# A linear layer and a product of squares by one level of Strassen, in a kernel whose order a planner writes

## The chip, the cores and the metric

One core of one Trainium2 chip. The time is device microseconds of one execution; the kernel before takes 1416.3 us as the median of three runs (1412.21 to 1417.54). Engines are named as in the profile: PE (TensorE), DVE (VectorE), ACT (ScalarE), POOL (GpSimd) and SP (SyncE, which issues most DMAs).

## The reference

A factorization machine: a linear layer plus half the sum, over 64 embeddings, of the square of a product minus the product of the squares. All in fp32; x is 1024 x 512, weight 64 x 512 x 512.

```python
out_lin = x @ lin_w.T + lin_b
xv = jnp.einsum('bf,efm->bem', x, weight)
zp = jnp.einsum('bf,efm->bem', jnp.square(x), jnp.square(weight))
interaction = 0.5 * jnp.sum(jnp.square(xv) - zp, axis=1)
return out_lin + interaction
```

Nearly all the work is `xv`, 64 products of 1024 x 512 by 512 x 512. `zp` summed over e is one product only: the squares of x by the sum over e of the squared weights.

## The kernel before

The 512 output columns are cut into groups of 16, 16 and then twenty times 24; with 64 embeddings a column a group is 1024 or 1536 wide. For each group the product of x and the weights is done by Strassen's method in the form of Winograd, on two levels. The outer level takes seven products, in the order 1, 6, 5, 2, 7, 4, 3; each is again cut, by `tree` into seven products of two matmuls, or, for the products 1, 5 and 7 of the wide groups, by `wide_tree` into twenty products of 3 x 3 cells. Names that the profile's rows use: `X1` to `X7` are the sums of x for the outer products, made once at the head by copies (ACT) and sums; `w11`, `w12`, `w21`, `w22a`, `w22b` are the quarters of a group's weights, `T1a`, `T1b`, `T2` their outer sums (made by DMAs of POOL that add), `t` the inner sums of weights (POOL, L421); `oa` to `od` hold the results of outer products, `p5`, `p53` those of inner ones. `b1`, `b3`, `b2_0` and `b2_1` are four PSUM buffers of two banks (the profile leaves out numbers and shows `b`; `_l` and `_r` are their halves). A product leaves a bank by DVE, which adds another term (L421), or by a copy of ACT (L431), often into another bank in which a further product is added: such a copy must be done before that product begins.

Beside these products ACT squares each finished output (L438) and DVE sums it over the embeddings (L447) into `acc`. In the same way each quarter of the weights is squared into `wsq` and summed into `w2_sum`; the two halves of a quarter are two loads of SP (L452), two squares and two sums.

Around that: at the head the linear layer, 32 matmuls of 128x512 (L503), goes to `lin_dram`; at the end the product of -x²/2 (L916, on DVE) with `w2_sum`, 32 matmuls of 128x512 (L950), is added to acc and the linear part (L930, L421) and stored.

Nothing of the order is written by hand. Every step is added to `Plan` with a cost on its engine; for PE a key gives a preferred place. `Plan.order` makes due times backward from the products, moves them by the table `AHEAD_OF` (signs of steps with eighths of a microsecond), and then deals out the steps forward in a time of its own: each engine takes the one that is ready and due first. Each engine then works strictly in this order. The even and the odd wide groups share their signs, so the order repeats every two groups, 124.8 us.

## Time and profile before

| | |
|---|---|
| Median of three runs | 1416.3 us (1412.21 to 1417.54) |
| The profiled execution | 1415.96 us, span 1414.2 us, granted clock 0.997 |
| PE busy | 1396.6 us (99%) |
| POOL busy | 1173.7 us (83%) |
| DVE busy | 1100.0 us (78%) |
| ACT busy | 806.0 us (57%) |
| Moved by DMA | 251.76 MB, mean 178 GB/s |

A row of the timeline gives the start in us, the length, the engine, the line of the kernel, the operation, out<-in, shapes and the number of records; in brackets the idle time just before it and what ended that. A matmul in fp32 leaves two records. PEld is the load of the stationary operand, SPq and ACTq the DMA queues of these engines.

### The profile page before, as it was taken

What the parts mean: (1) busy time and instruction counts of PE and PEld (TensorE: products, weight loads), DVE (VectorE), ACT (ScalarE), POOL (GpSimd) and SP (SyncE); (2) the same over time, 40 slices, a digit from 0 to 9 for tenths busy, and PEclk for the clock granted to TensorE, in tenths of its full rate; (3) what the DMA queues carried; (4) which work ended last, traced back from release to release, by engine and by line L of the source; (5) the groups of instructions that cost most, each with busy time, mean ns of one, the idle gap of its engine ahead of it and who ended that gap; (6) DMA issues with size and microseconds to landing.
All of it is one profiled execution on the core that took longest, in us unless ns stands there. A gap on an engine that the chain in (4) does not pass through costs nothing.

```text
span 1414.2 us, 16647 instructions
## 1 busy us (share of the span) xinstructions
PE 1396.6 (99%) x5160; PEld 971.5 (69%) x5160; DVE 1100.0 (78%) x1461; ACT 806.0 (57%) x1293; POOL 1173.7 (83%) x1117
## 2 busy tenths in 40 slices
PE   8999989999999999999999999999999999999998
PEld 3887757767776766767676676777677677767663
DVE  2678678878878786887879688787968878796895
ACT  1456465656757465665656566565746556574642
POOL 5999978897979798797979879897987989788870
PEclk9999999999999999999999999999999999999999
DMA  8589596777949676795968678596958859694773
GB/s 260 164 192 227 135 202 153 165 188 161 228 120 228 160 178 171 167 223 117 230 159 192 160 180 208 131 222 146 216 143 195 197 132 221 135 238 109 163 193 112
DMA packets 92599, 251.76 MB, mean 178 GB/s; under 512 B 29472, under 2 KB 30496, under 8 KB 92512
## 3 DMA queue, kind: packets, MB, share of 16 engines
q0 software_dynamic: 26448, 134.49, 49.6%
q1 hardware_dynamic: 65488, 115.17, 24.0%
q8 instruction: 42, 0.69, 0.2%
q10 hardware_dynamic: 576, 1.05, 0.2%
q14 instruction: 45, 0.37, 0.1%
HBM read 127.04 MB, written 6.19 MB: 94 GB/s over the span
## 4 chain that ended last, share of the span: by engine, by line
PE 90%; POOL 4%; DMA 4%; DVE 1%; issue 1%; ACT 0%; SPq 0%; POOLq 0%; DVEq 0%; ACTq 0%
PE b L464 51%; PE b_r L464 18%; PE b_l L464 17%; POOL t L421 2%; PE b_r L950 1%; PE b_l L950 1%; DMA oc<-od 1%; DMA T<-T1a 1%; DMA oa<-xT 1%; PE b_l L503 1%; PE b_r L503 1%; DMA w<-weight 1%; POOL X L421 1%; DMA X<-xT 0%; POOL ob L456 0%
## 5 line engine op out<-in xcount | busy, mean ns | idle before, releaser
L464 PE MATMUL b<-t,X 128*128 128x384 f32 (+1 forms) x1504 | 518.5, 474 | 1.9 <-DVE ob L421 1.1
L464 PEld LDWEIGHTS b<-t,X 128*128 128x128 f32 x1504 | 276.1, 190 | 168.4 <-DVE oa L421 18.8
L421 POOL TENSOR_TENSOR t<-t,w 128x256 f32<-128x256 f32 (+1 forms) x200 | 232.6, 1287 | 9.0 <-PE b L464 5.7
L421 POOL TENSOR_TENSOR t<-w 128x768 f32<-128x768 f32 (+1 forms) x88 | 163.0, 1860 | 88.1 <-PE b_l L464 70.5
L438 ACT ACTIVATE oa<-oa 128x768 f32<-128x768 f32 (+1 forms) x176 | 142.8, 822 | 134.5 <-DVE oa L421 132.4
L464 PE MATMUL b<-w,X 128*128 128x384 f32 (+1 forms) x576 | 193.9, 469 | 0.1
L464 PE MATMUL b_l<-t,X 128*128 128x256 f32 x720 | 189.6, 381 | 3.9 <-ACT b_l L431 3.9
L464 PE MATMUL b_r<-t,X 128*128 128x256 f32 x600 | 167.9, 383 | 0.4 <-DVE ob L421 0.3
L447 DVE TENSOR_REDUCE acc<-oa 128x12 f32<-128x768 f32 (+1 forms) x176 | 161.6, 920 | 3.7 <-ACT oa L438 3.7
L447 DVE TENSOR_REDUCE w_sum<-wsq 128x12 f32<-128x768 f32 (+1 forms) x176 | 161.5, 920 | 1.1 <-ACT wsq L438 1.0
L464 PEld LDWEIGHTS b_l<-t,X 128*128 128x128 f32 x720 | 137.2, 191 | 32.2 <-ACT b_l L431 4.5
L464 PEld LDWEIGHTS b<-w,X 128*128 128x128 f32 x576 | 109.1, 190 | 56.5 <-ACT p L431 2.1
L464 PEld LDWEIGHTS b_r<-t,X 128*128 128x128 f32 x600 | 113.9, 191 | 47.7 <-issue 5.0
L438 ACT ACTIVATE wsq<-w 128x768 f32<-128x768 f32 (+1 forms) x132 | 107.3, 821 | 38.8 <-DVE w_sum L447 16.9
L421 DVE TENSOR_TENSOR oa<-b,oa 128x768 f32<-128x768 f32 (+1 forms) x88 | 82.0, 932 | 59.6 <-PE b L464 55.7
L421 POOL TENSOR_TENSOR t<-w,t 128x384 f32<-128x384 f32 (+1 forms) x96 | 107.7, 1122 | 2.4
L431 ACT COPY b<-b 128x768 f32<-128x768 f32 (+1 forms) x94 | 71.2, 757 | 60.3 <-PE b L464 58.0
L464 PE MATMUL b_r<-w,X 128*128 128x256 f32 x400 | 99.8, 380 | 0.0
L464 PE MATMUL b<-T,X 128*128 128x384 f32 (+1 forms) x264 | 91.3, 477 | 0.6 <-DMA T<-T1a 0.6
L421 DVE TENSOR_TENSOR oa<-b,oc 128x768 f32<-128x768 f32 (+1 forms) x66 | 61.2, 930 | 34.7 <-PE b L464 32.9
L464 PEld LDWEIGHTS b_r<-w,X 128*128 128x128 f32 x400 | 76.3, 191 | 14.3
L421 POOL TENSOR_TENSOR oc<-ob,p 128x512 f32<-128x512 f32 (+1 forms) x80 | 82.3, 1105 | 3.6 <-ACT p L431 2.0
(143 smaller groups left out, 2618.1 us busy)
## 6 DMA issues: line engine op xcount, KB each, us to landing
w<-weight SPq DMA_DIRECT2D x120, 384.0 KB, 6.0
ob<-od POOLq DMA_DIRECT2D x40, 768.0 KB, 7.9
oc<-od POOLq DMA_DIRECT2D x40, 768.0 KB, 9.5
T<-weight SPq DMA_DIRECT2D x40, 384.0 KB, 4.0
w<-T POOLq DMA_DIRECT2D x20, 768.0 KB, 6.5
T1a<-weight SPq DMA_DIRECT2D x20, 384.0 KB, 3.3
w22a<-weight SPq DMA_DIRECT2D x20, 384.0 KB, 8.8
T1a<-weight POOLq DMA_DIRECT2D x10, 768.0 KB, 11.9
```

The costliest lines, as they stand in the source:

```text
L421: return f(o.ap, a.ap, b.ap)
L431: return nc.scalar.copy(o.ap, i.ap)
L438: lambda _: nc.scalar.activation(o.ap, i.ap, AF.Square), i.atoms, o.atoms)
L447: nc.vector.tensor_reduce(o, x, axis=AX.X, op=ALU.add)
L464: nc.tensor.matmul(a.ap, b.ap, w.ap, start=start, stop=True, skip_group_check=True)
L503: nc.tensor.matmul(o[j].ap, x.ap[:, ts((g * 2 + j) % (NB // 2), P)], w.ap, start=(k == 0), stop=(k == NK - 1),)
L950: nc.tensor.matmul(z.ap, view(xe[h, k // KH])[:, k % KH, ts((g * 2 + j) % (NB // 2), P)], reg("w2_sum", k * M, M).ap, start=(k == 0), stop ...
```

## The change

Both the linear layer and the last product are cut by one level of the same scheme: seven products of eight matmuls of 128x256 instead of 32 of 128x512 (`outer_products`, `big`). The sums of lin_w are made by DVE and those of `w2_sum` by POOL; the sums of x for the linear layer are those that the groups need anyway, of which X5 and X7 are now put on DVE (POOL made them before). The squares of x move from DVE to ACT, the adding of acc and of the linear part goes by quadrants, and five stores replace eight. Two copies from bank to bank by ACT stand in each `outer_products`. The loads of lin_w go through the queue of ACT in quarters, those of x through SP, and the second half of x no longer through ACT.

Four matmuls of zeros (`WARM`), from a DVE memset, stand at the start of PE's order.

In the planner loads share one line with the adding DMAs (`queue`), with less cost for both; copies and squares cost ACT less. The table has new numbers. The rings `p5` and `p53` keep their two buffers.

```diff
+HALF = 0.5 ** 0.5
+WARM = 4
+P5S = 2
+P53S = 2
 AHEAD_OF = """
-0:l 1:hvhc 2:3bp 3:hvw0 4:37v 5:338 6:3g7 7:34e 8:1o 9:33e a:33f b:-d c:369 d:-2 e:28 f:1 g:-1v h:-k i:-2k
...
+0:-1d 1:28mt 2:1rdw 3:28qb 4:28sp 5:1rhs 6:1r1z 7:1o2z 8:r13 9:1ny7 a:3m5 b:1qhi c:1nqc d:1okx e:1qxc f:m62
...
-        plan.add({ACT: 0.19 + 0.00083 * o.size}, emit, i.atoms, o.atoms,
+        plan.add({ACT: 0.06 + 0.00083 * o.size}, emit, i.atoms, o.atoms,
                  banks=i.banks(False) + o.banks(True))
 
     def square(o, i):
-        plan.add({ACT: 0.22 + 0.00083 * o.size},
+        plan.add({ACT: 0.10 + 0.00083 * o.size},
                  lambda _: nc.scalar.activation(o.ap, i.ap, AF.Square), i.atoms, o.atoms)
 
     def reduce(o, i, writes):
-    def dma(o, i, reads, writes, cost=2.4, land=1.5, queue=nc.sync):
-        plan.add({SP: cost}, lambda _: queue.dma_start(o, i), reads, writes, land=land)
+    def dma(o, i, reads, writes, moves=1.3, land=1.8, queue=nc.sync):
+        plan.add({SP: 0.4}, lambda _: queue.dma_start(o, i), reads, writes, land=land, queue=moves)
 
     def dma_add(o, i, rows, reads, writes):
         def emit(_):
             nc.gpsimd.dma_start(o, i, accum_op=ALU.add)
 
-        plan.add({POOL: 1.0}, emit, reads + writes, writes, land=2.0, queue=3.1 * rows / 1024)
+        plan.add({POOL: 0.7}, emit, reads + writes, writes, land=1.8, queue=2.5 * rows / 1024)
...
-    for k in range(NK):
-        q, r = divmod(k, KH)
-        for h in range(2):
-            o = x_in(h, q, r)
-            dma(o.ap, x_src[:, k, ts(h, H)], (), o.atoms, 1.2, 2.0,
-                nc.sync if h == 0 else nc.scalar)
-        o = reg("ob", KH * H + k * M, M)
-        dma(o.ap, lw_src[:, k, :], (), o.atoms, 1.2, 2.0)
-
...
+    C = M // 2
+    lw_in(0, 0, nc.scalar)
+    x_load(0, 0, nc.sync, 2)
+    lw_in(1, 0, nc.scalar)
+    x_load(0, 1, nc.sync)
+    lw_in(0, 1, nc.scalar)
+    lw_in(1, 1, nc.scalar)
+    x_load(1, 1, nc.sync)
+    x_load(1, 0, nc.sync)
+
+    def big(o, x, w, first, key, parts=((0, 0, 4), (1, 0, 4))):
+
+        for n, (k, j0, j1) in enumerate(parts):
+            outs = [reg(o, j * C, C) for j in range(j0, j1)]
+            xs = [Reg(x.tile, x.off + k * H + j * P, P) for j in range(j0, j1)]
+
+            def emit(_, k=k, outs=outs, xs=xs, j0=j0):
                 return [
-                    nc.tensor.matmul(
-                        o[j].ap, x.ap[:, ts((g * 2 + j) % (NB // 2), P)], w.ap,
-                        start=(k == 0), stop=(k == NK - 1),
-                    )
-                    for j in range(2)
+                    nc.tensor.matmul(a.ap, b.ap, w(k).ap, start=first and k == 0 and j % 2 == 0,
+                                     stop=True, skip_group_check=True)
+                    for j, (a, b) in enumerate(zip(outs, xs), j0)
                 ]
 
-            plan.add({PE: 2 * mm_cost(N)}, emit, x.atoms + w.atoms, reg(b).atoms,
-                     key=-1000 + 4 * k + g, banks=o[0].banks(True) + o[1].banks(True))
-    for g, b in enumerate(lin_banks):
-        name, off = ("oc", g * 2 * M) if g < 3 else ("w22b", 0)
-        for j in range(2):
-            tt(reg(name, off + j * M, M), bank(b, j), bias)
-        o = reg(name, off, 2 * M)
-        dma(lin_dram[:, ts(g, 2), :].rearrange("p a m -> p (a m)"), o.ap, o.atoms, (("lin", g),))
+            plan.add({PE: (j1 - j0) * mm_cost(C)}, emit,
+                     sum((r.atoms for r in (*xs, w(k), *outs)), ()),
+                     sum((r.atoms for r in outs), ()), key=key + 0.1 * n,
+                     banks=sum((r.banks(True) for r in outs), ()))
+
+    zero = reg("t", 0, P + N)
+    plan.add({DVE: 0.8}, lambda _: nc.vector.memset(zero.ap, 0.0), (), zero.atoms)
+    for n in range(WARM):
+        z, o = reg("t", 0, P), bank(f"b2_{n // 2}", n % 2)
+        zw = reg("t", P, N)
+        plan.add({PE: 1.8 * mm_cost(N)},
+                 lambda _, z=z, o=o, zw=zw: nc.tensor.matmul(o.ap, z.ap, zw.ap, start=True, stop=True),
+                 zero.atoms, o.atoms, key=-2000 + n, banks=o.banks(True))
+
...
+    tt(two(lsum[1]), lw(0, 1, (M, KH)), lw(0, 0, (M, KH)), only=DVE)
+    tt(two(lsum[2]), lw(1, 1, (M, KH)), two(lsum[1]), only=DVE)
+    tt(two(lsum[4]), lw(1, 0, (M, KH)), two(lsum[2]), only=DVE)
+    tt(two(lsum[7]), lw(0, 1, (M, KH)), lw(1, 1, (M, KH)), only=DVE)
...
-    tt(x_block(5), x_in(1, 1), x_in(1, 0), True)
+    tt(x_block(5), x_in(1, 1), x_in(1, 0), True, DVE)
     minus_both(x_block(6), x_block(5), x_in(0, 0))
-    tt(x_block(7), x_in(0, 0), x_in(1, 0), True)
+    tt(x_block(7), x_in(0, 0), x_in(1, 0), True, DVE)
     minus_both(x_block(3), x_in(0, 1), x_block(6))
+
+    def outer_products(xs, ws, base_key, ready, leave):
+
+        u2, u3, m4, m5 = "b2_0", "b1", "b3", "b2_1"
+        big("b1", xs[1], ws[1], True, base_key)
+        copy(pair(u2), pair("b1"))
+        big("b1", xs[2], ws[2], False, base_key + 1)
+        leave(0, 0, "b1")
+        big(m4, xs[4], ws[4], True, base_key + 2)
+        ready(0, m4)
+        big(m5, xs[5], ws[5], True, base_key + 3)
+        ready(1, m5)
+        big(u2, xs[6], ws[6], False, base_key + 4)
+        copy(pair(u3), pair(u2))
+        big(u3, xs[7], ws[7], False, base_key + 5)
+        leave(1, 0, u3)
+        leave(1, 1, u3)
+        big(u2, xs[3], ws[3], False, base_key + 6, ((0, 0, 2), (1, 0, 2), (0, 2, 4), (1, 2, 4)))
+        leave(0, 1, u2)
+
...
-                dma(o.ap, source(g, q)[:, k * iw:(k + 1) * iw], (), o.atoms, 2.4 * iw / 1024)
+                dma(o.ap, source(g, q)[:, k * iw:(k + 1) * iw], (), o.atoms, 1.3 * iw / 1024)
...
-        plan.add(
-            {DVE: 1.24},
-            lambda _, x=x: nc.vector.scalar_tensor_tensor(
-                x.ap, x.ap, -0.5, x.ap, ALU.mult, ALU.mult
-            ),
-            x.atoms, x.atoms,
-        )
...
+    x2 = {(h, q): next(rooms) for h, q in ((0, 0), (0, 1), (1, 1), (1, 0))}
+    for (h, q), x in x2.items():
+        dma(x.ap.rearrange("p (a m) -> p a m", a=KH), x_src[:, ts(q, KH), ts(h, H)], (), x.atoms)
+        plan.add({ACT: 0.10 + 0.00083 * x.size},
+                 lambda _, x=x: nc.scalar.activation(x.ap, x.ap, AF.Square, scale=HALF),
+                 x.atoms, x.atoms)
...
+    tt(two(zsum[1]), w2(0, 1), w2(0, 0))
+    tt(two(zsum[2]), w2(1, 1), two(zsum[1]))
+    tt(two(zsum[4]), w2(1, 0), two(zsum[2]))
+    tt(two(zsum[7]), w2(0, 1), w2(1, 1))
...
+    def ready(c, b):
+        if c == 0:
+            tt(rest[1, 0], rest[1, 0], pair(b), True)
+        else:
+            tt(rest[1, 1], rest[1, 1], pair(b))
+            tt(rest[0, 1], rest[0, 1], pair(b))
+
+    def leave(h, c, b):
+        r = rest[h, c]
+        n = 1 if (h, c) != (0, 1) else 2
+        for k in range(n):
+            o = Reg(r.tile, r.off + k * 2 * N // n, 2 * N // n)
+            tt(o, o, reg(b, k * 2 * N // n, 2 * N // n), c == 0)
+            dma(out_dst[:, 4 * h + k * 4 // n:4 * h + (k + 1) * 4 // n, ts(c, C)],
+                o.ap.rearrange("p (a m) -> p a m", m=C), o.atoms, ())
+
+    outer_products(xs, ws, 1e6, ready, leave)
```

The steps of the periodic part are the same, in another order. Three places of it:

PE in a periodic pair of groups, where the first wide tree begins: `b3_r` and `b3_l` take the tree's first products, ACT copies `b3_r` to `b2_1_l`, and the next `b3_r` waits for that. Before:

```order
L464 MATMUL b3_r<-t_81,X1_62 128x256 [waits DVE_49]
L464 MATMUL b3_l<-t_81,X1_62 128x256 [waits Pool_49]
L464 MATMUL b3_l<-t_81,X1_62 128x256
L464 MATMUL b2_0<-t_81,X3_64 128x384 [waits DVE_49]
L464 MATMUL b2_0<-t_81,X3_64 128x384
L464 MATMUL b3_r<-t_81,X1_62 128x256 [waits Activation_49,Pool_49]
L464 MATMUL b2_1_l<-t_81,X1_62 128x256 x2
```

and now:

```order
L472 MATMUL b3_r<-t_81,X1_62 128x256 [waits DVE_49]
L472 MATMUL b3_l<-t_81,X1_62 128x256 [waits Pool_49]
L472 MATMUL b3_l<-t_81,X1_62 128x256
L472 MATMUL b3_r<-t_81,X1_62 128x256 [waits Activation_49,Pool_49]
L472 MATMUL b2_1_l<-t_81,X1_62 128x256 x2
```

Two matmuls of another tree, 128x384, have moved out of the gap between the product and the matmul that waits for its copy.

ACT in the first wide group (`w_71` is w21; `wsq_86` and `wsq_87` are the two buffers that take its halves' squares). Before:

```order
L438 ACTIVATE wsq_87<-w_69 128x768
L438 ACTIVATE wsq_86<-w_69 128x768
L438 ACTIVATE oa<-oa 128x2x384
L438 ACTIVATE ob<-ob 128x2x384
L438 ACTIVATE wsq_87<-w_71 128x768
L431 COPY b_1_l<-b_r 128x512
L438 ACTIVATE oa<-oa 128x2x384
```

and now:

```order
L446 ACTIVATE wsq_86<-w_71 128x768
L446 ACTIVATE ob<-ob 128x2x384
L446 ACTIVATE oa<-oa 128x2x384
L439 COPY b_1_l<-b_r 128x512
L439 COPY p_0_82<-b_l 128x512
L439 COPY b_1_r<-b_l 128x512
L439 COPY p_0_82<-b_r 128x256
L446 ACTIVATE ob<-ob 128x2x384
L438 ACTIVATE oa<-b_r 128x256
L446 ACTIVATE ob<-ob 128x2x384
L439 COPY b_0_l<-b_1_l 128x512
```

The square directly ahead of the copy was one of w21, its second half; now a square of w21, its first half, stands three rows ahead of the copy, and that of the other half comes some rows behind the last one shown.

The end of PE's order and of DVE's after the change (`w2_sum` times squares of x; X2, X5 and w12 hold what is stored). PE:

```order
L529 MATMUL b2_0<-T1a_74,X6_67 128x256 x8
L529 MATMUL b1<-w11_69,X1_62 128x256 [waits DMAHW5_49,Activation_49,Pool_49]
L529 MATMUL b1<-w11_69,X1_62 128x256 x7
L529 MATMUL b2_0<-w2_sum_90,T1b_75 128x256 x6
L529 MATMUL b2_0<-w2_sum_90,T1b_75 128x256 [waits DVE_49]
L529 MATMUL b2_0<-w2_sum_90,T1b_75 128x256
```

and DVE:

```order
L429 TENSOR_TENSOR w12_70<-w12_70,b2_1 128x1024 [waits DVE_49]
L429 TENSOR_TENSOR w12_70<-w12_70,b1 128x1024 [waits DVE_49,PE_49,Activation_49]
L429 TENSOR_TENSOR X2_63<-X2_63,b2_0 128x512 [waits PE_49]
L429 TENSOR_TENSOR X5_66<-X5_66,b1 128x1024
L429 TENSOR_TENSOR X2_63<-X2_63,b2_0 128x512 [waits PE_49]
```

Before, 32 matmuls stood here and a DVE sum of 512 columns followed each four; now product 7 waits for a copy of the product just before it, and the last product's seventh matmul for DVE.

337 lines of the change are left out of this document (193 added, 144 removed).

## The prediction

> **What bounds the kernel now.** I read the busy shares and the chain of waits first, then the busy time in windows cut at the program's stages, then the groups of waits of TensorE, and last the timeline at each place where TensorE stands idle. From the page:
>
> ```profile
> PE 1396.6 (99%) x5160; PEld 971.5 (69%) x5160; DVE 1100.0 (78%) x1461; ACT 806.0 (57%) x1293; POOL 1173.7 (83%) x1117
> PE 90%; POOL 4%; DMA 4%; DVE 1%; issue 1%; ACT 0%; SPq 0%; POOLq 0%; DVEq 0%; ACTq 0%
> ```
>
> TensorE is busy for 1396.6 of 1414.2 us: 17.6 us of idle time are all that better waiting could win, beside shorter products. The windows say where they lie (each row: the window, its length, busy time of PE, PEld, DVE, ACT and POOL, the granted clock, the DMA share, GB/s):
>
> ```profile
> 0.00:36.00 36.00, 30.45 (x66) 13.37 (x67) 8.18 (x13) 6.73 (x8) 21.11 (x28) 1.00 0.83 257
> 60.00:120.00 60.00, 58.97 (x267) 49.69 (x267) 47.02 (x74) 33.08 (x58) 57.66 (x68) 1.00 0.84 198
> 120.00:180.00 60.00, 59.25 (x229) 42.53 (x228) 43.68 (x65) 34.60 (x62) 58.16 (x65) 1.00 0.72 171
> 180.00:200.00 20.00, 16.09 (x51) 11.07 (x50) 12.43 (x16) 10.45 (x17) 16.00 (x16) 0.83 1.01 227
> 300.00:424.80 124.80, 124.80 (x466) 87.18 (x464) 100.55 (x133) 75.20 (x120) 106.14 (x99) 1.00 0.75 179
> 424.80:549.60 124.80, 124.54 (x464) 86.82 (x463) 100.40 (x132) 74.95 (x120) 105.98 (x99) 1.00 0.75 179
> 1300.00:1380.00 80.00, 78.10 (x281) 52.29 (x280) 69.84 (x84) 43.49 (x68) 65.20 (x57) 1.00 0.79 186
> 1380.00:1414.00 34.00, 30.07 (x73) 13.36 (x71) 20.01 (x28) 6.94 (x9) 2.70 (x2) 0.99 0.37 108
> ```
>
> The periodic stage, two column groups in 124.8 us, is full: there is nothing to win but tenths, and much to lose. The idle time is at the head (5.5 us), in 180 to 200 (3.9), in the two start-up windows (1.0 and 0.75), shortly before the end (1.9) and after the last product (3.9). POOL, 97% busy from 60 to 180, is the engine that is late when the 180 to 200 stall begins. TensorE's waits by group (total, times, longest):
>
> ```profile
> PE b_l L503 <- DMA oa<-xT: 5.5, 1, 5.5
> PE b_l L464 <- ACT b_l L431: 3.9, 1, 3.9
> PE b L464 <- DVE ob L421: 1.1, 1, 1.1
> ```
>
> **The head.** The timeline of the first loads (start, length, engine, operation, records, the wait ahead of it):
>
> ```profile
> 5.50 2.05 PE L503 MATMUL b_l<-ob,oa 128*128 128x512 f32 x2 [5.50 <-DMA oa<-xT]
> 8.02 1.28 ACT L431 ACT_TABLE_LOAD   x1 [8.02 <-DMA oa<-xT]
> 9.31 1.04 ACT L431 COPY X<-oa 128x1024 f32<-128x1024 f32 x1
> 10.52 1.02 PE L503 MATMUL b_r<-ob,oa 128*128 128x512 f32 x2
> 11.38 1.02 PE L503 MATMUL b_l<-ob,oa 128*128 128x512 f32 x2
> 13.31 0.30 PEld L503 LDWEIGHTS b_l<-ob,oa 128*128 128x128 f32 x2 [0.88 <-DMA oa<-xT]
> ```
>
> An fp32 matmul leaves two records. At full speed one of 128x512 starts each 0.86 us (10.52 to 11.38); but from 5.50 to 10.52 only three ran, 5.02 us for 2.58, so the cold clock costs 2.44. The 32 matmuls take 32 x 0.858 = 27.4, with 2.44 and the wait at 13.31 (two slots after 11.38 is 13.10, so 0.2) 30.1: the linear layer ends at 35.6.
>
> After the change the same layer is 7 products of 8 matmuls of 128x256. One of those takes 0.43 (585.32 to 585.75 in the fence on copies below), so 56 x 0.432 = 24.2, 3.2 less. Two costs come with it. The order puts the first product's copy b2_0<-b1, 1024 wide, between product 1 and product 2, with no other product between: 1.04 (row 9.31) and about 0.3 of hand-over, 1.3 exposed. The copy ahead of product 7 has two tree matmuls (0.86) to hide behind: 0.5 exposed. So 26.0 from the first real matmul.
>
> When does that start? The zero matmuls need only a DVE memset of 640 columns, for which no row exists: at least 0.29 as the smallest DVE operation at the head, at most 0.9 by the sums of 512 and 768 columns (0.69 and 0.95 below). I take TensorE to begin at 1.2. If it warms as at 5.50, six records take 5.0, to 6.2, and the last two 0.86: 7.1. Its first half needs 384 KB (two loads on SP, one on ACT), where the matmul at 5.50 waits for 512; ACT, whose first work is at 8.02 today, has room to issue loads. Then the layer ends at 7.1 + 26.0 = 33.1: **-2.5**. The bounds: -0.5 if loads or the table load of 1.28 hold up the first copy, -4.2 if the real work starts at 5.5 warm.
>
> The Trainium skill, "TensorE: Matmul & The Clock Gate", section "Part 1: The HAM clock gate (the "warmup" mystery)", says half rate is the default, that about 3.4 us of activity open the gate and that an idle window of that length closes it. The closing agrees with the 3.91 us wait below; the opening took 5.0 here. By 3.4 the zero matmuls would end at about 6.4 and the sum would be 0.7 lower; the window of the page runs freely, so no one trace can settle it.
>
> DVE takes four sums of lin_w (0.69 each) and the X5 and X7 sums that POOL had; DVE is busy 8.18 of the first 36 us, so they fit, and POOL gets room.
>
> **The stall at 189.** Rows of POOL, SP, ACT and TensorE, and two windows:
>
> ```profile
> 179.61 1.73 POOL L421 TENSOR_TENSOR t<-w,t 128x384 f32<-128x384 f32 x1
> 181.37 0.33 SPq L452 DMA_DIRECT2D w<-weight  x1
> 191.34 0.84 ACT L438 ACTIVATE wsq<-w 128x768 f32<-128x768 f32 x1 [5.35 <-DMA w<-weight]
> 192.09 0.58 ACT L431 COPY b_l<-b_r 128x512 f32<-128x512 f32 x1
> 192.72 1.22 PE L464 MATMUL b_l<-t,X 128*128 128x256 f32 x2 [3.91 <-ACT b_l L431]
> 190.00:195.00 5.00, 2.28 (x5) 1.85 (x6) 1.53 (x2) 3.27 (x6) 4.92 (x6) 0.62 0.98 209
> 195.00:200.00 5.00, 5.00 (x17) 4.08 (x16) 2.00 (x4) 3.32 (x7) 1.08 (x2) 0.70 1.04 204
> ```
>
> POOL's sum ends at 181.34 and only then may SP load over the old w21. The DMA engines are full, so the load takes ten microseconds. In ACT's order the square of that half stands directly ahead of the copy that TensorE needs. TensorE loses 3.91, then runs at half clock: 2.28 x 0.38 + 5.00 x 0.30 = 2.4. Together **6.3**. In the new order the square ahead of this copy reads the first half of w21, which SP loads earlier and which waits for an earlier sum of POOL; the second half's square stands eleven rows later, behind the copies. So the copy no longer waits for the late load, and I take -6.3. The bounds: 0 if the first half too comes late behind full DMA queues (POOL is relieved of two sums at the head and of nothing else before 180), -6.3 if it is on time. A rest of about 1 us would leave the clock open, as the wait of 1.1 at 1334 does in a window with clock 1.00.
>
> **Copies in the periodic stage.** The new orders bring copies closer to their readers. Two examples of how near is near enough:
>
> ```profile
> 64.13 1.03 PE L464 MATMUL b<-w,X 128*128 128x256 f32 x4
> 64.33 0.69 DVE L421 TENSOR_TENSOR oc<-b,ob 128x512 f32<-128x512 f32 x1 [0.44 <-PE b L464]
> 65.08 1.13 PE L464 MATMUL b<-t,X 128*128 128x256 f32 x4
> 585.32 0.59 PE L464 MATMUL b_r<-t,X 128*128 128x256 f32 x2
> 585.75 1.03 PE L464 MATMUL b_l<-t,X 128*128 128x256 f32 x4
> 586.00 0.57 ACT L431 COPY b_l<-b_r 128x512 f32<-128x512 f32 x1 [0.72 <-PE b_r L464]
> ```
>
> A DVE evacuation of 0.69 with 0.86 us of products beside it lets TensorE go at 65.08 instead of 64.99: 0.09 lost, masked as busy time. An ACT copy of 0.57 ends at 586.57, and the slot after two products is 585.75 + 0.86 = 586.61: it would just fit. In the new order five of the six wide trees in a period have just that, 0.86 where there was 2.15; before, 13 DVE evacuations per period stood in a tight slot of 1.29, now 4. I take these against each other: 0 for ten periods, from -5 (each tight DVE slot is worth up to the 0.09) to +8 (the ACT copy late by 0.15 at each of some 50 trees). The start-up groups get some twenty slots of 0.86 on ACT where there were seven on DVE: **+0.5**, between 0 and 1.2.
>
> **The end.**
>
> ```profile
> 1331.91 1.23 DVE L916 SCALAR_TENSOR_TENSOR X<-X 128x1024 f32<-128x1024 f32 x1 [1.97 <-DMA X<-xT]
> 1333.05 0.95 DVE L421 TENSOR_TENSOR ob<-b,oa 128x768 f32<-128x768 f32 x1
> 1334.05 1.56 PE L464 MATMUL b<-t,X 128*128 128x384 f32 x4 [1.12 <-DVE ob L421]
> 1408.19 1.88 PE L950 MATMUL b_r<-w_sum,X 128*128 128x512 f32 x4
> 1410.11 0.69 DVE L421 TENSOR_TENSOR X<-b_r,X 128x512 f32<-128x512 f32 x1 [2.74 <-PE b_r L950]
> out<-X SPq DMA_DIRECT2D x4, 256.0 KB, 2.0
> lind<-oc SPq DMA_DIRECT2D x3, 512.0 KB, 2.9
> ```
>
> The wait at 1334 comes from a square of x that DVE waits for and does ahead of an evacuation. The change gives these squares to ACT, so this 1.1 should go; but DVE's additions of acc are now 1024 wide and the wait of ACT for the same loads has its own followers. I take -0.6 (-1.9 to +1).
>
> Now the last stage runs 32 x 0.858 = 27.4, then 0.2 to DVE, 0.69, and 3.4 from 1410.80 to the end: 31.7. After: 54 matmuls, 23.3, until the one that waits for DVE; the copy ahead of product 7, with nothing between, 1.3; then in the row of DVE 0.2, the first half of product 3 (0.69), a sum of 1024 (1.2 by the step from 0.69 to 0.95 per 256 columns), the last half (0.69); then 3.4, and up to 0.9 more since 512 KB leave just ahead of the last 256 (2.9 and 2.0 to landing). 30.8 to 31.7: **-0.5**, with the bounds -1.5 and +1. POOL's four sums of the squares' weights lie beside products (POOL is busy 2.70 of the last 34 us).
>
> **The sum.** -2.5 - 6.3 + 0 + 0.5 - 0.6 - 0.5 = -9.4 on the profiled execution's 1415.96, whose span is 1414.2 with 1.8 around it: 1406.6. That execution lies 0.3 under the median of 1416.3, which is within the spread of the runs. The planner's new costs for loads and additions change no instruction; they show only in the orders counted above.
>
> **The rivals.** *The stall stays, or moves* (0.22): the DMA share of 1.01 in 180 to 200 is not changed by an order, and all the same bytes must pass; against it, only one row of ACT stood in the way. Then -3.1: 1413.
>
> *Copies just in time become late* (0.13, the slower side): ACT works in order. If a square of 0.84 (row 191.34) starts just before the product ends, the copy comes up to 0.84 late, and in 50 trees a mean of 0.3 gives 15, of 0.5 gives 25: 1421 to 1432, say 1425. It decides from 0.19 a tree, where the 9.4 are gone. For it: five of six trees have this slot. Against it: ACT is busy 75 of 124.8.
>
> *All is hidden* (0.12): the real work starts at 5.5 on a warm clock, the tight DVE slots give their tenths back (-3): 1402.
>
> *The clock opens sooner* (0.08), by 3.4 us of activity instead of the 5.0 of this trace: the zero matmuls end at 6.4 and the rest is as forecast, 1405.9. The page named above states this.
>
> My forecast has 0.45, between 1402 and 1411.
>
> **The numbers.** A measurement of this kernel tells some 0.5% from no change: under 1409.2 is faster, over 1423.4 slower. Faster takes most of the forecast (0.40), the last two rivals (0.19) and a little of the first (0.02): 0.61. Slower is 0.09 out of the second. Same is 0.30. The range 1399 to 1417 takes in the first rival with its spread, leaves out nearly all of the slower one, and a little below.
>
> **What would show it.** Right: zero matmuls from about 1.2 us and full clock before 8; the first tree's matmuls some 2.5 us earlier; no wait over 1 us and no low clock between 180 and 200; the windows of 124.8 us still full, with the same number of records in each; a wait of about 1.3 <-ACT ahead of the seventh product in the last stage. Wrong: PE busy below 124 in a periodic window, or the waits list with ACT copies many times over; a stall at another load near 190 with a granted clock of 0.6; a first real matmul after 9 us.

## The result

The changed kernel takes 1430.5 us (median of four executions; 1429.6 to 1434.1) and the kernel before 1416.3 us (also of four; 1412.2 to 1417.5) on the same chip: a ratio of 1.011, interval 1.0083 to 1.0137. It is slower by 1.1%. The forecast was 1406.6 us, faster, with a range up to 1417. The profiled executions have spans of 1429.4 and 1414.2 us, 15.2 apart; everything below is about these 15.2.

From the page of the changed kernel, the busy shares and the chain of waits by engine:

```profile
PE 1406.8 (98%) x5264; PEld 986.0 (69%) x5264; DVE 1118.2 (78%) x1462; ACT 810.8 (57%) x1301; POOL 1178.4 (82%) x1121
PE 78%; DMA 8%; POOL 6%; DVE 4%; issue 3%; ACT 1%; SPq 0%; DVEq 0%; POOLq 0%; ACTq 0%
```

TensorE is "busy" for 10 us longer although its products got shorter. The chain is less of TensorE than before (78% instead of 90%), more of DMA, POOL and DVE. The windows of the prediction again, now of the changed kernel:

```profile
0.00:36.00 36.00, 32.67 (x127) 24.98 (x128) 24.19 (x23) 11.76 (x15) 21.73 (x29) 1.00 0.82 249
60.00:120.00 60.00, 58.77 (x261) 47.84 (x259) 45.02 (x71) 31.66 (x58) 57.80 (x70) 1.00 0.87 203
120.00:180.00 60.00, 58.11 (x227) 42.17 (x226) 44.37 (x65) 34.32 (x62) 53.56 (x56) 1.00 0.71 166
180.00:200.00 20.00, 20.00 (x74) 13.54 (x73) 18.35 (x22) 15.11 (x24) 17.76 (x17) 1.00 1.04 231
300.00:424.80 124.80, 124.44 (x460) 85.76 (x459) 99.64 (x131) 74.07 (x120) 104.37 (x96) 1.00 0.74 174
424.80:549.60 124.80, 124.50 (x457) 85.05 (x456) 99.43 (x131) 74.22 (x119) 104.55 (x98) 1.00 0.74 176
1300.00:1380.00 80.00, 78.23 (x290) 53.99 (x289) 65.54 (x83) 45.27 (x72) 70.99 (x64) 1.00 0.70 174
1380.00:1414.00 34.00, 29.39 (x113) 22.00 (x112) 32.65 (x31) 12.09 (x15) 11.28 (x9) 0.95 0.53 114
```

Two rows tell most. The window 180 to 200 is now full (20.00 of 20, clock 1.00): the stall is gone. The two windows of the periodic stage read 124.44 and 124.50, nearly full as before, but hold 460 and 457 records instead of 466 and 464: each matmul still looks busy while it waits a tenth, so the number of records tells the loss and the busy time hides it. Of TensorE's waits by group:

```profile
PE b L529 <- DVE ob L429: 4.6, 1, 4.6
PE b L529 <- ACT b L439: 1.3, 2, 1.1
```

The 4.6 us for DVE's `ob` did not exist before.

To see where the 15.2 us come from, I compared the times at which the two traces have issued the same amount of tree work (the matmul records of the trees' line, each counted at its undisturbed step: 0.216 us for 256 columns, 0.322 for 384). The same trees are computed in both, so the difference is how far the changed kernel lies behind; its steps are set beside the terms of the prediction's sum (work done is read at the last record that starts before the mark):

| stretch (us of tree work done) | behind at its end | step | forecast |
|---|---|---|---|
| head, to 20 | -0.1 | -0.1 | -2.5 |
| first groups, to 140 | +2.9 | +3.0 | +0.5 |
| the place of the stall, to 155 | -3.7 | -6.6 | -6.3 |
| rest of the start-up, to 260 | -3.1 | +0.7 | (in the +0.5) |
| periodic stage, to 1256 | +8.2 | +11.3 | 0 |
| the wait at 1334, to 1305 | +8.1 | -0.1 | -0.6 |
| the end | +15.2 | +7.1 | -0.5 |

So the periodic stage and the end lost 18 us, where the forecast had 0 and a gain of 0.5.

### The profile page after: what moved, and what is told of

The parts are those of the page before. It is cut to its first block, busy times and chain, and to the rows that moved or that the text cites. A ratio compares the mean times of both kernels' runs of the same rounds, so it can differ in the third digit from the quotient of the medians.

```text
span 1429.4 us, 16910 instructions
## 1 busy us (share of the span) xinstructions
PE 1406.8 (98%) x5264; PEld 986.0 (69%) x5264; DVE 1118.2 (78%) x1462; ACT 810.8 (57%) x1301; POOL 1178.4 (82%) x1121
## 4 chain that ended last, share of the span: by engine, by line
PE 78%; DMA 8%; POOL 6%; DVE 4%; issue 3%; ACT 1%; SPq 0%; DVEq 0%; POOLq 0%; ACTq 0%
PE b L472 44%; PE b_r L472 16%; PE b_l L472 16%; POOL t L429 4%; DMA ob<-od 2%; DMA oc<-od 2%; PE b L529 2%; DMA w<-T 1%; DVE acc L455 1%; POOL X L429 1%; DVE oa L429 1%; DMA oa<-xT 0%; DMA T<-weight 0%; DVE ob L429 0%; DMA w<-weight 0%
## 5 line engine op out<-in xcount | busy, mean ns | idle before, releaser
L472 PEld LDWEIGHTS b<-t,X 128*128 128x128 f32 x1504 | 280.2, 190 | 160.1 <-issue 9.2
L429 POOL TENSOR_TENSOR t<-w 128x768 f32<-128x768 f32 (+1 forms) x88 | 162.0, 1841 | 104.3 <-issue 77.3
L429 POOL TENSOR_TENSOR t<-t,w 128x256 f32<-128x256 f32 (+1 forms) x200 | 230.3, 1243 | 10.8 <-PE b L472 6.9
L455 DVE TENSOR_REDUCE w_sum<-wsq 128x12 f32<-128x768 f32 (+1 forms) x176 | 158.6, 919 | 4.1 <-ACT wsq L446 3.8
L472 PEld LDWEIGHTS b_l<-t,X 128*128 128x128 f32 x720 | 134.2, 190 | 30.9 <-ACT b_l L439 6.8
L472 PEld LDWEIGHTS b_r<-t,X 128*128 128x128 f32 x600 | 109.8, 190 | 59.1 <-issue 9.0
L429 DVE TENSOR_TENSOR oa<-b,oa 128x768 f32<-128x768 f32 (+1 forms) x88 | 82.1, 932 | 56.9 <-PE b L472 56.5
L439 ACT COPY b<-b 128x768 f32<-128x768 f32 (+2 forms) x98 | 75.7, 772 | 56.5 <-PE b L472 33.3
L429 POOL TENSOR_TENSOR t<-w,t 128x384 f32<-128x384 f32 (+1 forms) x96 | 96.8, 1008 | 2.0
L446 ACT ACTIVATE ob<-ob 128x768 f32<-128x768 f32 (+1 forms) x88 | 72.5, 825 | 36.9 <-DVE ob L429 26.2
L446 ACT ACTIVATE oc<-oc 128x768 f32<-128x768 f32 (+1 forms) x88 | 68.9, 819 | 39.2 <-DMA oc<-od 39.1
```

Source lines behind the costliest of these rows:

```text
L429: return f(o.ap, a.ap, b.ap)
L439: return nc.scalar.copy(o.ap, i.ap)
L446: lambda _: nc.scalar.activation(o.ap, i.ap, AF.Square), i.atoms, o.atoms)
L455: nc.vector.tensor_reduce(o, x, axis=AX.X, op=ALU.add)
L472: nc.tensor.matmul(a.ap, b.ap, w.ap, start=start, stop=True, skip_group_check=True)
```

## The experiments

"Behind" below is always measured as in this table, against the kernel before. In kernels whose order is written out as a list, the line numbers of the helpers are 201 higher (L429 is L630, L529 is L730, L576 is L777, L1043 is L1244).

**The new order without Strassen.** The kernel before, with the planner's new prices and, for the column groups, the new table of numbers.

```diff
-        plan.add({ACT: 0.19 + 0.00083 * o.size}, emit
+        plan.add({ACT: 0.06 + 0.00083 * o.size}, emit
...  (the other prices and the table's numbers of the column groups likewise)
```

> The kernel before with the new costs and, for the column groups, the new table; linear layer and last product as before. Theory (order): the stall near 190 is gone (-6.3), the periods lose 11 more, the start-up 2 to 3 more: 1421 to 1425, slower than before. Rival (order harmless): 1409 to 1411.

Measured: 1442.2 us, ratio 1.0195 (1.0179 to 1.021). The place of the stall, which comes 15 us later in this kernel, and a periodic window:

```profile
195.00:215.00 20.00, 19.64 (x73) 13.26 (x71) 17.79 (x23) 15.82 (x25) 13.95 (x14) 1.00 1.05 235
300.00:424.80 124.80, 124.80 (x463) 86.59 (x462) 99.91 (x132) 74.80 (x120) 105.39 (x98) 1.00 0.75 179
```

The stall goes with the order alone (-6.0 in that stretch). The periodic stage loses 9.3 us (12.4 behind at 260, 21.8 at 1256) with none of the new arithmetic in the kernel: the loss there comes with the order, not with Strassen. The start-up falls 15 us back (from -0.7 at 20 to +14.9 at 140; waits of 3.0 us for POOL's sums of x and 2.9 for an ACT copy), since this order was laid out behind another head; so this total says nothing on the whole change.

**Strassen without the new order.** The changed kernel, with the old prices and the old table for the column groups.

```diff
-        plan.add({ACT: 0.06 + 0.00083 * o.size}, emit
+        plan.add({ACT: 0.19 + 0.00083 * o.size}, emit
...
```

> The changed kernel, but with the old costs and, for all column groups, the old table: both Strassen products, the zero matmuls and the loads stay. Theory (the order costs the time): the eight periods lose 6.6 us between records as before and not 17.9, so about 11 us less; the start-up loses 3 less; the stall near 190 may be back (+6.3); 1416 to 1424. Rival (the Strassen products and their traffic cost it, the order is harmless): 1428 to 1432.

Measured: 1435.0 us, ratio 1.0146 (1.0109 to 1.0182), above both values expected. The start-up is 8.0 us behind at 140, and the periodic stage loses its 12.2 us in three jumps (5.1, 1.2 and 6.3 us in three stretches of 125) and nothing in the other five. Five untouched periods agree with the run above, that the old order itself is sound there. But the planner has made one long order from a different start, and its own misfits cover what was to be measured: as a test of the sum this run is inconclusive.

**The old order from 300 us on, behind the new head.** To get rid of the planner's reaction, I wrote the order out: the changed kernel's up to 300 us of planned time, then the kernel before's, with the new last stage at the same distance from the end.

```diff
-    for op, engine in plan.order():
+    planned = {op.n: (op, engine) for op, engine in plan.order()}
+    for op, engine in (planned[int(n, 36)] for n in SEQ.split()):
```

> The changed kernel in its own order up to the stage where the periods begin, and from there in the order of the kernel before (its end: that of the change, put in at the same distance from the last products). Theory (two orders, two prices: the new start-up is the better one behind this head, the new periods are the worse ones): each of the eight periods loses 0.8 us between records and not 1.5 to 3.2, about 11 us less: 1418 to 1421. Rival (what the periods lose comes with the state that head and start-up leave, as the run with the old table at the start-up suggests by its losses of 5 in two periods): losses of several us stay in some periods, 1424 to 1431.

Measured: 1417.8 us against 1415.2, ratio 1.0016 (1.0006 to 1.0025). A window of the periodic stage:

```profile
424.80:549.60 124.80, 124.80 (x466) 87.16 (x465) 100.57 (x133) 74.95 (x121) 106.27 (x99) 1.00 0.75 179
```

466 records again, and from 260 to 1256 us of work it loses 0.5 us instead of 11.3. This settles that the periodic stage's loss is its order. (Behind it, between 1256 and 1305, this kernel loses 3.9 us, by a DVE sum that takes 5.58 us; the run with all edits below shows the same place.) What in the order? Two late matmuls of the changed kernel (start, length, engine, operation, records, the wait ahead):

```profile
332.52 0.59 PE L472 MATMUL b_r<-t,X 128*128 128x256 f32 x2
332.95 1.03 PE L472 MATMUL b_l<-t,X 128*128 128x256 f32 x4
333.20 0.57 ACT L439 COPY b_l<-b_r 128x512 f32<-128x512 f32 x1
333.92 0.67 PE L472 MATMUL b_r<-t,X 128*128 128x256 f32 x2
355.20 0.57 ACT L439 COPY b_l<-b_l 128x512 f32<-128x512 f32 x1 [0.24 <-DVE oa L429]
355.82 0.51 PEld L472 LDWEIGHTS b_l<-w,X 128*128 128x128 f32 x3 [0.32 <-ACT b_l L439]
355.83 0.70 PE L472 MATMUL b_l<-w,X 128*128 128x256 f32 x2
```

In the first, ACT copies as soon as the product is there (333.20 to 333.77); four records of 0.216 behind 332.95 the next pair could go at 333.81, and goes at 333.92, and its own length is 0.67 instead of 0.59; the row names nothing as the end of a wait. In the second the row names the copy as what ended the wait: it ends at 355.77, the matmul starts at 355.83, and its pair takes 0.70. So such a slot loses about 0.1 for the wait and up to 0.1 behind it; both recur in each of the eight periods. Counted over the two orders in 300 to 1298 us of planned time, 512-wide copies with only 0.86 us of products between producer and reader number 40 now and none before, where the least was 1.29. In the traces over the same stretch, 155 records start 0.03 us or more late and lose 16.8 us together; before, 56 lost 5.3. How the 11.5 us between divide stays open: of the 16.8, 5.3 lie at records that start within 0.14 us behind the end of an ACT operation, or right behind such a record (none did before), and 4.5 lie in the same way at ends of POOL operations alone (1.0 before); but near is no proof, and for many of the others no end of any engine is near. The planner's price for a 512-wide copy went from 0.19 + 0.42 = 0.61 us to 0.48, below the 0.57 of the rows. That this made the slots tight is likely, but was not tried by itself: with another price the whole order comes out different.

**Two zero matmuls instead of four**, in the head:

```diff
-lambda _, z=z, o=o, zw=zw: nc.tensor.matmul(o.ap, z.ap, zw.ap, start=True, stop=True),
+(lambda _, z=z, o=o, zw=zw: nc.tensor.matmul(o.ap, z.ap, zw.ap, start=True, stop=True)) if n < 2 else None,
```

> The changed kernel with two zero matmuls (those into b2_0) and not four. Theory (the head is bound by ACT: the loads that it issues, its table load at 8.90 and the copies behind it): the second product still starts at 12.6, the time is the same within 1 us. Rival (the zero matmuls' warming decides): the real matmuls start earlier on a cold clock and the second product moves by more than 1 us, either way.

Measured: 1431.4 us, ratio 1.0116 (1.0101 to 1.0132), and at 20 us of work the same place as with four (within 0.2 us of the kernel before in both). The head of the changed kernel:

```profile
1.59 2.07 PE L548 MATMUL b_l<-t 128*128 128x512 f32 x2 [1.59 <-DVE t L543]
7.89 3.62 PE L529 MATMUL b<-ob,oa 128*128 128x256 f32 x16
11.27 0.29 DVE L576 SCALAR_TENSOR_TENSOR X<-X 128x128 f32<-128x128 f32 x1 [9.73 <-ACT X L439]
11.55 1.00 ACT L439 COPY b<-b 128x1024 f32<-128x1024 f32 x1 [0.31 <-PE b L529]
12.60 1.99 PE L529 MATMUL b<-ob,oa 128*128 128x256 f32 x8 [1.09 <-ACT b L439]
13.87 1.10 DVE L429 TENSOR_TENSOR T1b<-ob,w22b 128x512 f32<-128x512 f32 x1
15.02 3.72 PE L529 MATMUL b<-T1b,ob 128*128 128x256 f32 x16 [0.43 <-DVE T1b L429]
```

and with two zero matmuls:

```profile
5.16 4.78 PE L529 MATMUL b<-ob,oa 128*128 128x256 f32 x16
9.03 1.28 ACT L439 ACT_TABLE_LOAD   x1 [9.03 <-DMA ob<-xT]
10.33 1.04 ACT L439 COPY X<-oa 128x1024 f32<-128x1024 f32 x1
11.28 1.01 ACT L439 COPY b<-b 128x1024 f32<-128x1024 f32 x1
12.34 2.00 PE L529 MATMUL b<-ob,oa 128*128 128x256 f32 x8 [2.40 <-ACT b L439]
```

Real work starts 2.7 us earlier, on a slow clock (16 records in 4.78 us instead of 3.62), and is done at 9.94. It gains 0.26 at product 2, for the copy that this product waits for stands in ACT's order behind the table load and a copy of x, which wait for a load until 9.03. Nothing of that is left at the product that needs DVE's sum `T1b`: it starts at 15.14 here and at 15.02 with four. DVE's sums of lin_w stand behind an operation that waits for ACT's first copy (11.27 above), so they come no earlier. So in these two kernels the clock does not set the length of the head; ACT's first operations and the DVE sums behind them do.

**POOL's sums of the last stage on DVE**:

```diff
-    tt(xs[5], xs[4], x2[1, 0], True)
+    tt(xs[5], xs[4], x2[1, 0], True, DVE)
...
-    tt(two(zsum[1]), w2(0, 1), w2(0, 0))
+    tt(two(zsum[1]), w2(0, 1), w2(0, 0), only=DVE)
...  (xs[7], zsum[2], zsum[4], zsum[7] likewise)
```

> The changed kernel with the four sums of w2_sum and the sums X5 and X7 of the last product on DVE instead of POOL. Theory (an addition of DVE on SBUF stood still for 5.6 us while POOL did four sums one behind the other): the addition of 928 columns takes 1.1 to 2.5 us and not 6.7, the wait of 4.6 before the last product and the half clock behind it go: 1423 to 1426. Rival (DVE is simply full near the end): DVE has 5 us more to do, the wait stays or grows: 1430 to 1436.

The reason for it are these rows of the changed kernel, POOL and DVE ahead of TensorE's wait of 4.61:

```profile
1380.97 1.56 POOL L429 TENSOR_TENSOR T1b<-w_sum,T1a 128x512 f32<-128x512 f32 x1
1382.10 6.69 DVE L1043 SCALAR_TENSOR_TENSOR X<-T,X 128x928 f32<-128x928 f32 x1
1382.26 2.02 POOL L429 TENSOR_TENSOR oa<-oa,oc 128x768 f32<-128x768 f32 x1
1384.02 1.49 POOL L429 TENSOR_TENSOR w<-w_sum 128x512 f32<-128x512 f32 x1
1385.25 2.55 POOL L429 TENSOR_TENSOR X<-w22a,X 128x1024 f32<-128x1024 f32 x1
1392.43 1.81 DVE L429 TENSOR_TENSOR ob<-b,ob 128x768 f32<-128x768 f32 x2
1393.43 3.45 PE L529 MATMUL b<-w_sum,w22a 128*128 128x256 f32 x8 [4.61 <-DVE ob L429]
1395.89 1.11 DVE L1043 SCALAR_TENSOR_TENSOR w<-w,w 128x928 f32<-128x928 f32 x1
```

Additions of the same shape take 1.11 us at 1395.89 and 6.69 at 1382.10, where POOL runs four sums back to back; the long one ends 1.0 us after POOL's last. Behind it, DVE's evacuation `ob` is late, TensorE waits 4.61 us, and its clock falls (eight records of 256 in 3.45 us instead of 1.89). Measured with the sums on DVE: 1428.4 us, ratio 1.0093 (1.0076 to 1.011), between the two values expected. The addition takes 1.12 us, and the 4.6 are gone; but with six more sums DVE is itself late earlier (one of them, at 1366.65, meets a POOL sum and takes 1.64 us, and another of this size, at 1353.80, takes 0.68 with none ahead of it), and TensorE waits 2.21 us for an ACT copy at 1369.9 and runs at a lower clock behind it. The planner has also moved some products and copies near the end, so the run is no clean move of six sums. The theory on the long addition holds; as a repair it moves the loss.

**The addition moved instead**, DVE's order (names as in the changed kernel, X_63 is the accumulated part):

```diff
-SCALAR_TENSOR_TENSOR X_63<-T_76,X_63 128x4x232
 TENSOR_REDUCE acc_89<-oa 128x2x6
 SCALAR_TENSOR_TENSOR T1b<-T1a,X_67 128x1024
...
 TENSOR_TENSOR ob<-ob,b 128x2x384
+SCALAR_TENSOR_TENSOR X_63<-T_76,X_63 128x4x232
```

> The changed kernel in its own order, with one instruction moved: DVE's addition of 928 columns of acc stands behind POOL's sums for the last product instead of beside them. Theory (this one addition stood still while POOL's sums ran): it takes 1.1 to 1.3 us and not 6.7, the wait of 4.6 and the half clock behind it go: -6, 1424 to 1425. Rival (another instruction of DVE meets the same sums): another one takes 4 us or more, 1428 to 1431.

Measured: 1427.6 us, ratio 1.0081 (1.0065 to 1.0096). The addition takes 1.11 us at its new place. But the next DVE operation with both inputs in SBUF takes its place:

```profile
1381.80 5.93 DVE L777 SCALAR_TENSOR_TENSOR T1b<-T1a,X 128x1024 f32<-128x1024 f32 x1
1390.37 2.78 PE L730 MATMUL b<-w_sum,w22a 128*128 128x256 f32 x8 [2.72 <-DVE ob L630]
```

**Both moved behind POOL's sums**:

```diff
-SCALAR_TENSOR_TENSOR X_63<-T_76,X_63 128x4x232
-TENSOR_REDUCE acc_89<-oa 128x2x6
-SCALAR_TENSOR_TENSOR T1b<-T1a,X_67 128x1024
...
+SCALAR_TENSOR_TENSOR X_63<-T_76,X_63 128x4x232
 SCALAR_TENSOR_TENSOR w_70<-w_71,w_70 128x4x232
+SCALAR_TENSOR_TENSOR T1b<-T1a,X_67 128x1024
```

> The changed kernel in its own order, with only two instructions of DVE moved: the 928-column addition of acc (as in the run that moved it alone) and the sum of product 3 (T1b<-T1a,X, 128x1024), both behind POOL's run of sums. Alone, the first gave 1427.6, since the second then stood still for 5.93 us. Theory (the loss at the end is DVE's two-input sums standing still beside POOL's sums, whichever comes first): both take 1.1 to 1.2 us, the wait of 2.7 us for DVE's ob at about 1390 and the half clock behind it go, and 1430.5 falls by the tail's 7.1 us to 1423.5, 1421.5 to 1425.5, ratio to before 1.004 to 1.0065; what stays over before is start-up and periods. Rival (the late evacuation ob comes from the dense order of DVE's own work there): 1427 to 1430.

Measured: 1424.5 us, ratio 1.0072 (1.0056 to 1.0087), as the theory had it. Both are short (1.12 and 1.22 us), and no wait for `ob` is left:

```profile
1389.21 1.12 DVE L1244 SCALAR_TENSOR_TENSOR X<-T,X 128x928 f32<-128x928 f32 x1
```

The end now loses 0.8 us against the kernel before instead of 7.1: two instructions of one engine, moved by a few places, are 6 us.

**The order of the last products.** Product 5 placed between product 6 and product 7, which waits for product 6's copy, and the last additions behind all matmuls:

```diff
 MATMUL b2_0<-T1a_74,X6_67 128x256 x8
+MATMUL b1<-w11_69,X1_62 128x256 x8
 MATMUL b2_0<-w2_sum_90,T1b_75 128x256 x8
```

> The changed kernel in its own order, with two moves in the last product: product 5 stands between product 6 and product 7, so that the copy from bank to bank has 3.45 us to hide behind; and the additions behind product 7 and 3 stand behind all matmuls, the one of 1024 first. Theory: the waits of 1.1 and 0.8 in the last product go and the last store is a quarter behind a free queue: -2 to -3, 1427 to 1429. Rival (DVE, with two additions of 1024 now late, sets the end): 1430 to 1431.

Measured: 1430.0 us, ratio 1.0099 (1.0084 to 1.0114). The two waits that the prediction had put into the last products were there in the changed kernel, 1.34 us (foreseen 1.3) for the copy and 0.94 (0.2 + 0.69 in the prediction's row of DVE) ahead of the last product's seventh matmul; here both are gone, and the time from 1324 us of work to the end falls from 25.8 to 23.9 us. The medians differ by only 0.5 us, at the value of the rival, so that most of these 2.0 is seen in the profile alone.

**All three edits**: the order from 300 on, the moved addition and the order of the last products together.

> All three together: the old order of the periods, the addition behind POOL's sums, the two moves in the last product. Theory: the gains add up, -11 - 6 - 2.5: 1410 to 1412, which is under the kernel before. Rival (the gains are given back at the end, where the old periods meet another end): 1415 to 1420.

Measured: 1415.6 us, ratio 0.9998 (0.9989 to 1.0007): no gain over the kernel before, as the rival had it. One place holds it:

```profile
1353.33 5.55 DVE L777 SCALAR_TENSOR_TENSOR X<-X,w22a 128x1024 f32<-128x1024 f32 x1
1360.74 3.78 PE L673 MATMUL b_r<-w,X 128*128 128x256 f32 x8 [3.87 <-ACT b_r L639]
```

It is again a DVE sum of two SBUF inputs beside POOL sums: at 1290 us of work this kernel lies 3.6 us ahead of the kernel before, at 1305 1.3 us behind.

**That sum moved**, ten places later in DVE's order, to where POOL's queue has a gap:

```diff
-SCALAR_TENSOR_TENSOR X_67<-X_62,w22a 128x1024
 TENSOR_REDUCE acc_89<-oa 128x2x6
...
 TENSOR_TENSOR oc<-ob,b_1_r 128x256
 TENSOR_REDUCE acc_89<-oa 128x2x6
+SCALAR_TENSOR_TENSOR X_67<-X_62,w22a 128x1024
```

> The kernel with all three edits, with one instruction of one engine moved: DVE's sum of product 6 (X<-X,w22a, 128x1024, two inputs in SBUF) stands ten places later in DVE's order, where POOL has nothing queued. There it took 5.55 us in the run with all edits, against 1.2 elsewhere, and TensorE waited 3.87 us at 1360.74 and ran at half clock behind it (about 6.7 us lost in all). Theory (DVE's sum stands still while POOL works off its queue of sums, and everything behind it on DVE is late): the sum takes 1.2 us, the wait at 1360 goes and with it the half clock, 1415.6 - 6.7 = 1409 us, 1407 to 1411, ratio to before 0.993 to 0.997. Rival 1 (ACT's copy was late for a reason of its own, DVE's sum only ran beside it): 1415.6 stays, 1414 to 1417. Rival 2 (the long sum holds POOL up at its new place, or a later two-input sum meets POOL instead): a wait of 2 to 4 us turns up somewhere else in 1360 to 1400, 1412 to 1416.

Measured: 1415.9 us, ratio 1.0009 (0.9999 to 1.0019), the second rival. The wait at 1360 is gone and the sum takes 1.22 us. With everything 5 us earlier, the next one meets POOL:

```profile
1369.18 7.69 DVE L777 SCALAR_TENSOR_TENSOR T1b<-T1a,X 128x1024 f32<-128x1024 f32 x1
1380.38 3.52 PE L730 MATMUL b<-w_sum,w22a 128*128 128x256 f32 x8 [4.73 <-DVE ob L630]
```

**Both sums moved**, this one too, behind the additions:

```diff
-SCALAR_TENSOR_TENSOR T1b<-T1a,X_67 128x1024
 TENSOR_TENSOR ob<-b_1,ob 128x2x384
...
 SCALAR_TENSOR_TENSOR w_70<-w_71,w_70 128x4x232
+SCALAR_TENSOR_TENSOR T1b<-T1a,X_67 128x1024
```

> The run before with one more instruction of DVE moved: the sum of product 3 (T1b<-T1a,X, 128x1024, two inputs in SBUF) behind the two 928-column additions of acc, as in the run with two sums late. In the run before it met POOL's sums at 1369.18 and took 7.69 us; TensorE waited 4.73 us for DVE's ob at 1380.38 and ran at half clock behind it, and its place against the kernel before went from 3.99 us ahead (at tree work 1305) to 4.06 behind (at 1324). Theory (DVE's two-input sums stand still beside POOL's queue, and nothing else is wrong at the end): both sums take 1.1 to 1.3 us, no wait of more than 1 us is left between 1340 and 1400, and 1415.85 falls by 8.05 us to 1407.8, 1406 to 1410, ratio to before 0.993 to 0.997. Rival (one of the later two-input sums, the 928-column additions or the 1024-column ones, meets POOL in its turn): a new wait of 2 to 5 us, 1411 to 1416.

Measured: 1408.5 us (1408.3 to 1410.0) against 1414.5, ratio 0.9958 (0.9944 to 0.9971), within the theory's range: 0.4% faster than the kernel before. The sums, and the two windows of the end:

```profile
1361.34 1.22 DVE L777 SCALAR_TENSOR_TENSOR X<-X,w22a 128x1024 f32<-128x1024 f32 x1
1379.70 1.22 DVE L777 SCALAR_TENSOR_TENSOR T1b<-T1a,X 128x1024 f32<-128x1024 f32 x1
1300.00:1380.00 80.00, 80.00 (x289) 53.63 (x288) 64.36 (x82) 47.43 (x72) 70.33 (x62) 1.00 0.78 182
1380.00:1414.00 34.00, 23.07 (x105) 19.58 (x104) 21.06 (x24) 6.64 (x8) 1.81 (x1) 0.95 0.29 83
```

From 1300 to 1380 TensorE is now busy for the whole 80 us. The steps against the kernel before, as in the table: 0.1 at the head, +2.1 in the first groups, -6.6 at the place of the stall, +2.0 in the rest of the start-up, +0.6 in the periodic stage, -1.6 at the wait of 1334 and -2.6 at the end. So the gain at the stall, which alone is more than this kernel's whole lead, comes from the new order. Strassen in the linear layer won nothing at the head, and the end, with the last product in seven, won 2.6; what the two are worth in a sound order of their own no run shows, since the one without the new order was inconclusive.

## Why the prediction was wrong

**The stall at 189: right.** Forecast -6.3, measured -6.6, and for the reason given: the square that stood ahead of the copy no longer waits for the late load. The run with only the new order shows it too. The rival by which the stall stays is out.

**The periodic stage: the step that failed.** The prediction held the end of a copy, 586.57, against the next slot, 586.61, found that it "would just fit", and set the tight ACT slots against the looser DVE slots: 0, up to +8. Measured +11.3. Left out was the hand-over from ACT to TensorE, 0.06 to 0.15 us in the rows above (355.77 to 355.83; 333.77 to 333.92, if the copy is what that matmul waited for), and the 0.1 that the first matmul behind a wait takes longer. In the first slot shown the copy starts 0.25 behind the products' start and takes 0.57; with the hand-over that is 0.88 to 0.97, and the slot is 0.86. The prediction had this side as its slower rival, "copies just in time become late", at 0.13, and its point of decision, 0.19 a tree, was passed: the copies with so short a slot number 40 in this stage, and 11.3 over 40 is 0.28, if all of it is theirs. What it argued there, a square that ACT has just begun, is not what the rows above show. For the whole loss only the order is shown as the cause; how much of it lies in these slots stays open.

**The end: the second step that failed.** The prediction put POOL's four sums "beside products", at no cost, and got -0.5; measured +7.1. What those sums lie beside is DVE's operations with two SBUF inputs, and these stand still. The rows above show it four times (6.69, 5.93, 5.55 and 7.69 us for 1.1 to 1.2), with three different instructions as the victim, and taking the victims away from POOL's sums takes the loss away: the end then costs +0.8 with two sums moved late, and -2.6 with both sums moved in the old periods. Rows of the kernel before would have told it, POOL and DVE at its end:

```profile
1367.36 1.42 POOL L421 TENSOR_TENSOR t<-w22b,t 128x384 f32<-128x384 f32 x1
1367.84 1.97 DVE L930 SCALAR_TENSOR_TENSOR X<-X,X 128x976 f32<-128x976 f32 x1
1368.73 1.93 POOL L421 TENSOR_TENSOR t<-w,t 128x384 f32<-128x384 f32 x1
1373.20 1.17 DVE L930 SCALAR_TENSOR_TENSOR T1b<-w,T1b 128x976 f32<-128x976 f32 x1
```

One shape, 1.17 us where no sum of POOL was running and 1.97 beside its sums: here DVE waits for the first sum to end, works, and holds up the second (1.93, where the same form takes 1.00 at 1370.63). A stretched row next to a plain one of the same shape was the sign, and the prediction looked at neither. The Trainium skill states the rule ("SBUF — State Buffer", section "SBUF: two separate sides"): VectorE and GpSimd share one pair of ports as an exclusive lock, held for the whole instruction of the one that starts first, and a VectorE operation with two SBUF inputs takes part in it against a GpSimd operation that reads SBUF. The rows just shown agree. But by that a wait lasts one sum, and at 1382.10 it lasted until the fourth had ended. The planner knows of the conflict too: operations flagged `both` are kept away from POOL's in planned time. The addition of `acc` has no flag; the sums that suffered have it, and met POOL since the real times had drifted from the plan.

**The head: mis-sized.** Forecast -2.5, measured -0.1. The zero matmuls did as foreseen, real work began at full clock at 7.89 (forecast 7.1), and the copy ahead of product 2 cost about the 1.3 that it was given. The prediction let the length follow from there. The term that was too small is DVE's sums of lin_w, put at 0.69 each and at no wait: the three up to `T1b` took 1.21, 1.11 and 1.10 us, one behind the other, began only behind ACT's first copy, and held TensorE up at 15.02 (0.43 us idle, and the matmul starts 0.59 later than its slot). It is the loss of the end on a small scale: these sums have two inputs in SBUF too, and each ends 0.54 to 0.55 us behind the end of a POOL sum of x that had begun before it (at 12.14, 13.28 and 14.42), where a sum of this size took 0.68 with none ahead of it. A wait of 0.7 for a sum of POOL at 38.04 was not in the working either. The prediction had the table load ahead of the first copy only as a bound (-0.5); with two zero matmuls, real work at 5.16 gives the same head. The rivals that rested on an earlier start (*all is hidden*, *the clock opens sooner*) would then have won little by it; a start as early on a full clock was not tried.

**The first groups: mis-sized.** Forecast +0.5, measured +3.0 to 140 and +0.7 more to 260, in many tenths at tight slots like those of the periodic stage, and two waits of about 1 us. No run took these apart; the fastest kernel above still has them.

**The small terms.** The copy ahead of product 7 and the last product's wait measured about what was foreseen. The wait at 1334 went, as foreseen, but the stretch around it won only 0.1 in all where 0.6 was forecast.

That the fastest kernel, 1408.5 us, lies near the forecast of 1406.6 is luck: its head won nothing and its start-up lost 4.1 where -2.5 and +0.5 were forecast, and its last two stretches won 4.2 where 1.1 was.

## What to carry to other kernels

A slot that "just fits" by the lengths of rows does not fit: look in the trace for the shortest distance between a product and the reader of its copy that runs undisturbed, and take that as the limit (the order before kept 1.29 us for a copy of 0.57; at 0.86 the rows shown lost 0.2). Before work is given to POOL, list DVE's operations with two SBUF inputs around it and look whether one of them is already stretched; a run of POOL sums whose rows overlap held such an operation for the whole run here, and moving one of them may only hand the wait to the next. In a stage that is full, compare the number of records in a window and not the busy time, which counts short waits as work.

## What the runs showed of the hardware

How long DVE's operation waits was not expected. In the rows at 1382.10 each POOL sum starts ahead of its predecessor's recorded end (1382.26 against 1380.97 + 1.56 = 1382.53; 1384.02 against 1384.28; 1385.25 against 1385.51), and DVE gets no turn until the last has ended. In the kernel before, at 1367.84, the next sum starts only 0.05 ahead of the end (1368.73 against 1368.78), and DVE gets in between. It is so in all thirteen traces, for every two-input operation of DVE that was held by 0.3 us or more: none got in between two sums whose rows overlap by 0.24 us or more, and each got in at the first end where the next sum's row overlaps by 0.05 or less. That takes in a sum of x at the head, `X<-oa`, which the change gave to DVE: 4.53 us at 22.83 beside four such POOL sums, and 4.50 to 4.53 in all ten kernels with this start-up order; what it costs there was not looked at. Where the row that overlaps is a DMA issue of POOL, both happened: DVE got no turn in the run with one sum moved (at 1369.60, overlap 0.33), and it got one in the run without the new order (at 1389.67, overlap 0.37). What makes the rows overlap was not tried, and POOL's spans are rough.

It was not expected either how short a wait lets the clock fall, where the prediction went by some 3.4 us of idling: with the sums on DVE, 2.21 us were enough, and the granted clock was 0.73 in the 4 us from 1372 on:

```profile
1369.89 1.24 PE L472 MATMUL b_r<-w,X 128*128 128x256 f32 x4 [2.21 <-ACT b_r L438]
1372.00:1376.00 4.00, 4.00 (x13) 3.13 (x13) 2.19 (x4) 0.67 (x2) 0.27 (x2) 0.73 0.00 0
```

So at the end of this kernel a late evacuation costs TensorE more than its wait: in the run with one sum moved, the stretch with the wait of 4.73 lost 8.1 us in all.
